# Reordering parts of a hand-scheduled two-layer kernel: gram blocks of the second image, softmax sums, transposes, and identity products at the start

## The chip, the cores and the metric

The kernel runs on one core of one Trainium2 chip. The metric is the device time of one execution in microseconds (us); a figure for a kernel is the median of several runs. TensorE (PE) multiplies, its weight loads (PEld) overlap the products, VectorE (DVE) does elementwise work and statistics, ScalarE (ACT) does exponentials and copies, GpSimd (POOL) does some elementwise work, and SyncE (SP) issues nearly all DMAs in order.

## What is computed

The input x has shape 8 x 768 x 32 x 32, in float32: eight images of 768 channels and 1024 pixels. Two layers follow each other, each with a group norm (`_gn`) ahead of it and a residual sum behind it.

```python
x = x + _L0_conv_ref(_gn(x), W_qkv, W_proj, b_proj)   # layer 0
x = x + _L1_conv_ref(_gn(x), conv_w, conv_b)          # layer 1
...
# layer 0: 12 heads of 64
var_v = jnp.var(v, axis=-1, ddof=1, keepdims=True)
var_k = jnp.var(k, axis=-1, ddof=1, keepdims=True)
attn = softmax(var_v @ swapaxes(var_k) * scale)       # 1024 x 1024 per head
out = (attn @ v) @ W_proj.T + b_proj
...
# layer 1: 28 correlations of the normalised feature with shifts of itself, then a 1x1 convolution
corr = stack([sum(feat_pad[:, :, r:h+r, c:w+c] * feat_n, axis=1) for r, c in offsets])
out = einsum('bchw,oc->bohw', concat([feature, corr]), conv_w) + conv_b
```

The scores are the outer product of two vectors, so the attention matrix of a head is made by exponentials of one row, scaled by one number for each of 128 partitions.

## The kernel before

The program is written out as one static order of instructions for each engine. A planner inside the kernel, `Clock` (L73 to L126), keeps a planned time `now`, planned ends of ACT and DVE work, and a list of jobs with due times. `later.after(us, job)` makes a job due so long after now; `later.after_dve(us, job)` (L89) counts from the planned end of DVE's work. `pass_time` (L110) moves the plan on and emits the jobs that fall due. The plan decides only the order of emission; on the chip each engine runs its own list in that order and waits on semaphores.

**Stages.** For each image b: keys and values (`KeysValues`, 56 units of PE work of 12 matmul records each, L577), attention over six head pairs hp (`Attention`, `Pair`), projection (`project`, L1321), group norm, and layer 1 for the image before (`Corr`, `Conv`), which runs beside the attention of the next image. `work_off` (L1302) takes PE work from three lists: `rest` (key and value units, then convolution units), attention steps in fours, and `beside` (the gram blocks). An entry of `rest` is taken when its keys are in the set `ready`. A step of attention is four blocks t of `products` (L750, matmuls at L756, out tile `av`). Around each such group `next_to(beside)` (L1295) emits one gram block. If both halves of the values are there and the work left in `rest` is at most `TAIL` (L51, 14.0 planned us), that work is held back until attention is over (L1311).

**Softmax sums.** For some pairs (L38, `SUMMED`: pairs 0, 3, 4, 5 for image 0, and 3, 4, 5 for the others) DVE adds the exponentials (`acc`, two buffers of `bkpool`, L174), and PE sums `acc` over the partitions: `sum_up` (L782, tile `den`, L789), and for the last pair `sum_up_last` (L832), which takes reciprocals straight from PSUM in four pieces on DVE (`invert`, L845). For the other pairs ACT sums while it makes a second set of exponentials (`junk`, L741) from a row `bk` that is loaded over 128 partitions; after a summed pair this load is emitted once `bk_free` is set by `sum_up` (L793, L943). The next summed pair may not start before that either (L955).

**Rows for the exponentials.** `spread` (L663) makes the variances on DVE (`vm`, `km`); `values` (L679) then turns them by PE (tile `ptv`, L339), copies them on DVE (`rsv`), and stores them (`vdr`, L551). `rows` (L715) loads each row to 128 partitions (`bc<-vdr`, L720), and the exponentials read it (L731).

**Correlations.** `turn` (L1065) copies one block of the normalised image `f` on POOL (L1078) into the one buffer of `turnpool` (L176); `gram` (L1080) multiplies it with `f` (L1093, 24 records, tile `gr`), copies the result (`win`) and stores it (`windowed`). After blocks 3 and 7 `diagonals` (L1116), `scale` and `columns` take the shifted products from DRAM; `to_dram` (L1147) turns them (tile `ct`) and stores them (`rows<-cr`, L1159); `gather` (L1165) loads them with eleven DMAs into `cs` and `v` (L1170 to L1178). The products and a copy `cs<-cs` (L1187) follow. Some convolution units then get a matmul with `cs` added in the same PSUM bank, two at a time (`join`, L996; L1000). A bank is emptied by DVE (`take`, L1007).

For image 1 (b = 1 in the main loop, whose layer 1 is that of image 0) a fresh `Corr` is made and its first block is turned by the first `gram`. For later images `start_corr` (L1427) turns it ahead, near the end of the first half of keys and values. The gram blocks of b > 1 also get two extra places in `rest`, at indexes 3 and 7 (L1457 to L1458).

Of the kernel before, what the change touches and what calls it, by code (L numbers as in the profile page):

```python
# [6 lines left out]
F32 = mybir.dt.float32  # L7
# [6 lines left out]
P = 128  # L14
# [37 lines left out]
EXP, SUM, STEP_US = 1.07, 1.15, 1.73  # L52
KV_US, T_US, CORR_US = 1.93, 2.58, 1.2
GRAM_US = 1.4

# [100 lines left out]
def two_layers(ctx, tc, x, wkv, wproj, bproj, wconv, wcorr, bconv, out):  # L158
# [225 lines left out]
    sums0 = WeightSums(0, nc.sync, nc.scalar)  # L384
    ident = const.tile([P, P], F32, name="ident")
    make_identity(nc, ident)
    group = const.tile([P, P // 4, 4], F32, name="group")
    nc.gpsimd.memset(group, 0.25)
    for base, sign in ((0, 1), (3, -1)):
# [74 lines left out]
    class Norm:  # L464
# [35 lines left out]
                    nc.scalar.activation(high, high, AF.Identity, bias=shift, scale=self.rstd)  # L500
            ready.add(key)

        def apply(self, to, src, key, apart):


            def chunk(j):
                vector.tensor_scalar(to[:, j, :], src[:, j, :], self.mean, self.rstd, ALU.subtract, ALU.mult)
                if j + 1 < J:
                    later.after(apart, lambda: chunk(j + 1))
                else:  # L510
                    ready.add(key)

            chunk(0)

# [38 lines left out]
    class KeysValues:  # L553
# [109 lines left out]
        def spread(self, half):  # L663
            b = self.b
            name = f"{b}_{half}"
            km2 = st.tile([P, HH, MT], F32, tag="km2", bufs=2, name=f"km2{name}")
            head_m2(self.bn["k", half], km2, f"k{name}")
            top = st.tile([P, HH], F32, tag="top", name=f"top{name}")
            vector.tensor_reduce(top, km2, AX.X, ALU.max)
            most = st.tile([P, HH], F32, tag="most", name=f"most{name}")  # L670
            nc.gpsimd.partition_all_reduce(most, top, P, bass_isa.ReduceOp.max)
            m2 = st.tile([P, HH, MT], F32, tag="vm2", bufs=4, name=f"vm2{name}")
            head_m2(self.bn["v", half], m2, f"v{name}")
            nk = st.tile([P, HH, MT], F32, tag="nk", bufs=4, name=f"nk{name}")
            kdr, vdr = [dpool.tile([HH, N], F32, tag=f"{kind}dr", name=f"{kind}dr{name}") for kind in "kv"]
            for of, new in ((self.m2, m2), (self.nk, nk), (self.kdr, kdr), (self.vdr, vdr)):
                of.append(new)

            def values():  # L679
                to_rows(m2, vdr, f"v{name}")  # L680
                ready.add(("v", b, half))

            def keys():
                for h in range(HH):
                    vector.tensor_scalar(
                        nk[:, h, :], km2[:, h, :], most[:, h : h + 1], HD ** -0.5 / (HD - 1) ** 2,
                        ALU.subtract, ALU.mult,
                    )
                ready.add(("nk", b, half))
                if not set(SUMMED[b > 0]).issuperset(range(3 * half, 3 * half + 3)):  # L690
                    later.after_dve(0.5, rows)

            def rows():
                to_rows(nk, kdr, f"k{name}")
                ready.add(("k", b, half))

            later.after_dve(1.0 if b else 2.5, values)
            later.after_dve(2.2 if b else 3.5, keys)


    class Pair:
# [48 lines left out]
        def products(self, t):  # L750
            if t == 0:
                self.av = avp.tile([P, 2, HF], F32, tag="av", name=f"av{self.b}_{self.hp}")
            exs = self.exs.pop(t)
            for hf in range(2):
                for e in range(2):
                    nc.tensor.matmul(  # L756
                        self.av[e * HD : (e + 1) * HD, hf, :], lhsT=self.vt[:, t, e, :],
                        rhs=exs[e][:, hf * HF : (hf + 1) * HF], start=t == 0, stop=t == MT - 1,
                    )
            if t == MT - 1:  # L760
                later.after(STEP_US + 0.2, self.evacuate)
            if self.summed:
                before = list(self.first)
                if t == 0:
                    self.acc = [bkpool.tile([P, N], F32, tag="bk", name=f"acc{self.b}_{self.hp}_{e}") for e in range(2)]
                for acc, ex in zip(self.acc, exs):
                    if t:
                        vector.tensor_tensor(acc, before.pop(0) if t == 1 else acc, ex, ALU.add)
                self.first = exs
                if t == MT - 1:  # L770
                    later.after_dve(0.5, self.sum_up if self.hp < HP - 1 else self.sum_up_last)
            if t == MT - 1:
                self.over = True
                self.try_finish()
# [57 lines left out]
        def sum_up_last(self):  # L832

            dens = []
            for hf in range(2):
                at = slice(hf * HF, (hf + 1) * HF)
                den = other([P, HF], f"den{self.b}_{self.hp}_{hf}")
                for e in range(2):
                    nc.tensor.matmul(
                        den[e * HD : (e + 1) * HD, :], lhsT=ones, rhs=self.acc[e][:, at], start=True, stop=True  # L840
                    )
                dens.append(den)
            self.rd = self.acc[0]

            def invert(n):  # L845

                q = HF // 2
                vector.reciprocal(self.rd[:, n * q : (n + 1) * q], dens[n // 2][:, n % 2 * q : (n % 2 + 1) * q])
                if n < 3:
                    later.after_dve(1.5 if self.b else 0.0, lambda: invert(n + 1))  # L850
                else:
                    self.rd_at = clock.dve
                    self.try_finish()

            invert(0)

        def invert(self):
            self.inv = invs[self.hp % 2]
# [202 lines left out]
    class Corr:  # L1061
# [70 lines left out]
        def scale(self, hf, dd):  # L1132

            b = self.b
            m = st.tile([P, 4], F32, tag="m", name=f"m{b}_{hf}")
            vector.tensor_scalar(m, dd[:, :, 0], NORM_EPS2, None, ALU.max)
            rn = st.tile([P, 4], F32, tag="rn", name=f"rn{b}_{hf}")
            nc.gpsimd.tensor_tensor(rn, m, neghalf, ALU.pow)

            def columns():  # L1140
                dn = st.tile([P, 4, NROW], F32, tag="dn", name=f"dn{b}_{hf}")
                vector.tensor_copy(dn[:, :, 0], rn)
                for q in range(4):
                    vector.scalar_tensor_tensor(dn[:, q, 1:NROW], dd[:, q, :], rn[:, q : q + 1], mask, ALU.mult, ALU.mult)
                later.after_dve(0.7 if b else 4.0, lambda: to_dram(dn))

            def to_dram(dn):  # L1147
                pt = small(f"ct{b}_{hf}")
                columns, over = dn.rearrange("p q r -> p (q r)"), 4 * NROW - HD
                turned(pt[0:HD, 0:P], columns[:, 0:HD])  # L1150
                turned(pt[HD:P, 0:P], columns[:, over:])
                cr = work([P, P], f"cr{b}_{hf}")
                vector.tensor_copy(
                    cr.rearrange("k (y s x) -> k y s x", y=4, s=2),
                    pt[:, 0:P].rearrange("k (s y x) -> k y s x", s=2, y=4),
                )
                for q in range(4):
                    at, row = PAD + hf * HF + q * P, q * NROW + (HD - over) * (q == 3)
                    nc.sync.dma_start(out=rows[b % 2][:, at : at + P], in_=cr[row : row + NROW, :])  # L1159
                if hf == 1:  # L1160
                    later.after(3.0, self.gather)

            later.after_dve(2.5, columns)
# [138 lines left out]
    def work_off(rest, attention=None, beside=()):  # L1302
        while rest or (attention and not attention.over()):
# [14 lines left out]
            else:  # L1318
                clock.pass_time(0.5)

    def project(b, ots, held=None):  # L1321
        f = first_f[0] if b == 0 else image_tile(fpool, "f", f"f{b}")
        for n, us in ((0, 0.0), (1, 0.5), (3, 1.5), (4, 3.0), (2, 12.0), (5, 14.0)) if b else ():
# [22 lines left out]
        def apply(norm):  # L1346
            to = f if b + 1 < NB else image_tile(xnpool, "xn", "f_last")
            layer1.append((to, f))
            norm.apply(to, f, ("f", b), (2.0 if b else 1.0) if b + 1 < NB else 0.0)

        def spreads_and_apply():
            norms[0].spreads()
# [74 lines left out]
    def start_corr(b):  # L1427
        corrs.append(Corr(b, layer1[b][0]))
        corrs[-1].turn(0)
# [7 lines left out]
    for b in range(NB + 1):  # L1437
# [6 lines left out]
        if b:  # L1444
# [1 line left out]
            if b > 1:  # L1446
                clock.wait(*has_f, ready=ready)
            f, acc = layer1[b - 1] if b > 1 else first_f * 2
            corr = corrs[-1] if 1 < b < NB else Corr(b - 1, f)
            conv = Conv(  # L1450
                b - 1, f, None if b < NB else acc, (lambda b=b: next_image(b + 1)) if b + 1 < NB else lambda: None
            )
            grams = [(GRAM_US if t < MT - 1 else 0.9, has_f, lambda t=t: corr.gram(t)) for t in range(MT)]
            first, start = (0.0, has_f, conv.sums.first), (0.0, (), conv.start)
            if b < NB:
                beside = grams
                for n in (3, 7) if b > 1 else ():  # L1457
                    rest.insert(n, (0.0, has_f, lambda: next_to(beside)))  # L1458
                rest.insert(len(rest) - 4, (0.0, has_f, lambda: remaining(beside)))
                rest.insert(len(rest) - 4, first)  # L1460
# [63 lines left out]
```

## Time and profile before

| | us |
|---|---|
| median of 3 runs (lowest, highest) | 2656.82 (2652.53, 2659.18) |
| the profiled execution: its time | 2655.61 |
| its span, first to last instruction | 2653.9 |
| DVE, ACT, POOL busy | 1605.4, 1368.4, 414.3 |
| exponentials on ACT (L731), x768 | 828.8 |
| attention products on PE (L756), x3072 records | 701.1 |
| chain that ended last: share of PE | 91% |

One float32 matmul call shows as two records in the trace, and two records that fill 64 columns each run side by side. The number in brackets at the end of a row of the timeline is the time for which the engine stood idle ahead of that group, and what ended it; a row merges equal instructions that follow each other, and a row's start is that of its first. `SPq` rows are DMA issues, not transfers. The times of all rows are us from the start of the span.

### The profile page before, as it was taken

The page shows a single profiled execution, that of the slowest core. Times are in us where ns is not written, and L with a number is a line of the kernel's source. Part 1 is how long each engine was busy: PE and PEld are TensorE (multiplying, and loading weights), DVE is VectorE, ACT ScalarE, POOL GpSimd, SP SyncE. Part 2 cuts the span into 40 slices and gives each one's busy share as a digit, 9 for nine tenths or more (in the row PEclk, how much of TensorE's full clock was granted, in tenths as well). Part 3 has the DMA queues.
Part 4 walks back from the last instruction along what each step waited for, and adds up shares of the span by engine and source line. Part 5 has one row for each costly group of instructions (what it writes and reads, how often), then busy time and mean ns, then how long its engine had stood idle before and what let it go on. Part 6 is the DMA issues. An engine that isn't in the chain of part 4 may idle for free.

```text
span 2653.9 us, 40302 instructions
## 1 busy us (share of the span) xinstructions
PE 2602.3 (98%) x14694; PEld 1307.0 (49%) x14694; DVE 1605.4 (60%) x4110; ACT 1368.4 (52%) x1841; POOL 414.3 (16%) x444
## 2 busy tenths in 40 slices
PE   7999999899999999999999999999999999999999
PEld 3554565333674347633466334763347433575333
DVE  6858744676456854478544785348753577535864
ACT  1498069710498215981169801797018960189500
POOL 4320030003210033000430004300123001320000
PEclk9999999999999999999999999999999999999999
DMA  7864455455554555635556364562655526545333
GB/s 287 292 236 147 143 191 144 136 176 168 183 179 135 173 167 180 193 112 195 156 180 196 94 214 154 171 202 80 222 167 165 195 84 230 169 135 167 97 118 101
DMA packets 323391, 446.64 MB, mean 168 GB/s; under 512 B 59458, under 2 KB 245170, under 8 KB 323194
## 3 DMA queue, kind: packets, MB, share of 16 engines
q1 hardware_dynamic: 321962, 441.32, 51.6%
q8 instruction: 117, 1.92, 0.3%
q10 hardware_dynamic: 1232, 2.75, 0.3%
q14 instruction: 80, 0.66, 0.1%
HBM read 377.49 MB, written 64.40 MB: 167 GB/s over the span
## 4 chain that ended last, share of the span: by engine, by line
PE 91%; DMA 4%; DVE 2%; ACT 1%; issue 1%; SPq 1%; POOL 0%; DVEq 0%; POOLq 0%; ACTq 0%
PE x L336 36%; PE av L756 23%; PE y L336 18%; PE z L336 9%; PE gr L1093 3%; DMA x<-x1d 1%; PE den L789 1%; ACT ex L731 1%; PE x L1000 1%; PE y L1000 1%; DMA kv<-kvs 1%; PE z L1000 0%; DMA x1d<-f 0%; DVE x L152 0%; DMA xn<-in_x_dram 0%
## 5 line engine op out<-in xcount | busy, mean ns | idle before, releaser
L731 ACT ACTIVATE ex<-bc,nk 128x1024 f32<-128x1024 f32 x768 | 828.8, 1138 | 422.1 <-DMA bc<-vdr 258.9
L756 PE MATMUL av<-ex,v 128*64 128x512 f32 x3072 | 701.1, 597 | 11.1 <-ACT ex L731 11.1
L756 PEld LDWEIGHTS av<-ex,v 128*64 128x64 f32 x3072 | 322.1, 138 | 345.3 <-issue 206.2
L741 ACT ACTIVATE junk<-bk,vm 128x1024 bf16<-128x1024 f32 x368 | 420.5, 1143 | 31.6 <-DMA bk<-kdr 25.5
L152 DVE TENSOR_TENSOR acc<-acc,ex 128x1024 f32<-128x1024 f32 x300 | 344.6, 1211 | 0.0
L214 ACT COPY kp<-x 128x384 f32<-128x384 f32 x28 | 13.4, 478 | 565.7 <-PE x L336 556.9
L336 PE MATMUL y<-kv,s 128*64 128x384 f32 x1488 | 269.9, 487 | 0.0
L336 PE MATMUL x<-kv,xn 128*64 128x384 f32 x1512 | 265.7, 488 | 1.6 <-DVE xn L152 1.6
L336 PE MATMUL x<-kv,s 128*64 128x384 f32 x1488 | 259.3, 486 | 0.0
L336 PEld LDWEIGHTS x<-kv,xn 128*64 128x64 f32 x1512 | 144.0, 138 | 103.8 <-issue 82.7
L336 PEld LDWEIGHTS x<-kv,s 128*64 128x64 f32 x1488 | 144.2, 137 | 92.1 <-issue 68.8
L336 PEld LDWEIGHTS y<-kv,s 128*64 128x64 f32 x1488 | 140.0, 137 | 87.1 <-issue 68.6
L490 POOL TENSOR_TENSOR rstda<-vea,neghalf 128x1 f32<-128x1 f32 x8 | 4.8, 595 | 978.2 <-DVE vea L152 978.2
L1078 POOL TENSOR_TENSOR turn<-f,ones 128x384 f32<-128x384 f32 x112 | 111.0, 1011 | 257.2 <-PE gr L1093 177.0
L336 PE MATMUL z<-kv,xn 128*64 128x384 f32 x768 | 135.6, 486 | 0.0
L336 PE MATMUL x<-v,wt 128*64 128x512 f32 x576 | 131.1, 594 | 0.0
L336 PE MATMUL x<-f,wt 128*64 128x512 f32 x504 | 119.5, 593 | 0.0
L152 DVE TENSOR_TENSOR v<-y,v 128x128 f32<-128x128 f32 x180 | 41.0, 283 | 127.1 <-PE y L336 127.0
L594 POOL TENSOR_TENSOR s<-xn 128x384 f32<-128x384 f32 x64 | 67.4, 1062 | 285.3 <-PE x L336 192.0
L152 DVE BATCH_NORM_STATS2 vbn<-v 128x6 f32<-128x64 f32 x720 | 101.7, 210 | 0.0
L336 PEld LDWEIGHTS z<-kv,xn 128*64 128x64 f32 x768 | 75.9, 137 | 46.7 <-issue 35.7
L1093 PEld LDWEIGHTS gr<-f,turn 128*64 128x64 f32 x1344 | 90.2, 138 | 16.3 <-POOL turn L1078 5.8
(190 smaller groups left out, 2989.5 us busy)
## 6 DMA issues: line engine op xcount, KB each, us to landing
kv<-kvs SPq DMA_DIRECT2D x124, 576.0 KB
kv<-in_wkv_dram SPq DMA_DIRECT2D x95, 576.0 KB
bc<-vdr SPq DMA_DIRECT2D x96, 512.0 KB
f<-in_x_dram SPq DMA_DIRECT2D x48, 512.0 KB
bk<-kdr SPq DMA_DIRECT2D x46, 512.0 KB
x1d<-f SPq DMA_DIRECT2D x42, 512.0 KB
x<-x1d SPq DMA_DIRECT2D x42, 512.0 KB
out_dram<-x SPq DMA_DIRECT2D x82, 256.0 KB
```

The source lines that it names most:

```text
L152: return getattr(self.engine, name)(*args, **kw)
L214: nc.scalar.copy(to, at)
L336: nc.tensor.matmul(out[at], lhsT=lhsT[:, at], rhs=rhs, start=start, stop=stop, **kw)
L490: nc.gpsimd.tensor_tensor(self.rstd, ve, neghalf[:, 0:1], ALU.pow)
L594: nc.gpsimd.tensor_tensor(self.sums[g][:, 0], a[g][2], a[g][3], ALU.add)
L731: nc.scalar.activation(ex, self.bc[e], AF.Exp, scale=self.kv.nk[self.half][:, h, t : t + 1])
L741: nc.scalar.activation(junk, self.bk[e], AF.Exp, scale=self.kv.m2[self.half][:, h, t : t + 1], accum_out=self.sums[:, e, t : t + 1],)
L756: nc.tensor.matmul(self.av[e * HD : (e + 1) * HD, hf, :], lhsT=self.vt[:, t, e, :], rhs=exs[e][:, hf * HF : (hf + 1) * HF], start=t == 0, ...
L789: nc.tensor.matmul(den[at * 32 : (at + 1) * 32, :], lhsT=ones[:, 0:32], rhs=self.acc[e][:, hf * HF : (hf + 1) * HF], start=True, stop=True,)
L1000: nc.tensor.matmul(t, lhsT=wcorr_sb[at, i, :], rhs=cs[at, tokens, :], start=False, stop=True, skip_group_check=True)
L1078: nc.gpsimd.tensor_tensor(to[:, :, side], half, windows(ones, ones.ap[0], (0, J), (HW, 4), (1, HW)), ALU.mult)
L1093: nc.tensor.matmul(ps[side * HD : (side + 1) * HD, :n].rearrange("p (y x) -> p y x", x=WIDE), lhsT=block[:, j, side, :], rhs=image[:, 4 * ...
```

## The change

Eight edits, none of which adds or removes arithmetic of the result.

1. 36 matmuls of the identity with itself (128 x 128) into a scratch bank, right after the identity is made.
2. For image 0, the end of the normalisation of `f` (`Norm.apply`) calls `turn_first`: `start_corr(0)` turns gram block 0 on POOL, and six planned us later the key "turned" becomes ready. The gram blocks of b = 1 need that key besides `("f", 0)`.
3. The gram blocks of b = 1 get extra places in `rest`, at indexes 7, 11 and 15.
4. For image 0, `to_dram` is due 0.7 us behind DVE's work rather than 4.0.
5. For image 0 and pairs other than the last, `sum_up` is due 3.0 us behind DVE's work rather than 0.5.
6. For images after 0, the first reciprocal of the last pair is due 1.2 us after `sum_up_last` rather than at once.
7. For b > 1 and the second half of keys and values, `values` and `keys` are due 1.0 us later.
8. `corrs[-1]` becomes `corrs.pop()`, since the list is now also filled for image 0.

```diff
+WARM = 36
...
     make_identity(nc, ident)
+    warm = smp.tile([P, 512], F32, tag="sm", name="warm")
+    for n in range(WARM):
+        nc.tensor.matmul(warm[:, 0:P], lhsT=ident, rhs=ident, start=True, stop=True)
...
-        def apply(self, to, src, key, apart):
+        def apply(self, to, src, key, apart, then=None):
...
                     ready.add(key)
+                    if then:
+                        then()
...
-            later.after_dve(1.0 if b else 2.5, values)
-            later.after_dve(2.2 if b else 3.5, keys)
+            more = 1.0 if b > 1 and half else 0.0
+            later.after_dve((1.0 if b else 2.5) + more, values)
+            later.after_dve((2.2 if b else 3.5) + more, keys)
...
-                    later.after_dve(0.5, self.sum_up if self.hp < HP - 1 else self.sum_up_last)
+                    last = self.hp == HP - 1
+                    later.after_dve(0.5 if self.b or last else 3.0, self.sum_up_last if last else self.sum_up)
...
-            invert(0)
+            later.after(1.2 if self.b else 0.0, lambda: invert(0))
...
-                later.after_dve(0.7 if b else 4.0, lambda: to_dram(dn))
+                later.after_dve(0.7, lambda: to_dram(dn))
...
+    def turn_first():
+        start_corr(0)
+        later.after(6.0, lambda: ready.add("turned"))
...
-            norm.apply(to, f, ("f", b), (2.0 if b else 1.0) if b + 1 < NB else 0.0)
+            norm.apply(to, f, ("f", b), (2.0 if b else 1.0) if b + 1 < NB else 0.0, None if b else turn_first)
...
-            corr = corrs[-1] if 1 < b < NB else Corr(b - 1, f)
+            corr = corrs.pop() if 1 < b < NB else Corr(b - 1, f) if b == NB else None
...
-            grams = [(GRAM_US if t < MT - 1 else 0.9, has_f, lambda t=t: corr.gram(t)) for t in range(MT)]
+            grams = [(GRAM_US if t < MT - 1 else 0.9, has_f if b > 1 else has_f + ("turned",), lambda t=t: (corr or corrs[0]).gram(t)) for t in range(MT)]
...
-                for n in (3, 7) if b > 1 else ():
+                for n in (3, 7) if b > 1 else (7, 11, 15):
                     rest.insert(n, (0.0, has_f, lambda: next_to(beside)))
```

## The prediction, made before the changed kernel was run

> **What bounds the kernel now.** I read the page's busy shares first, then the list of who waited for whom on PE, then the timeline around each wait.
>
> ```profile
> PE 2602.3 (98%) x14694; PEld 1307.0 (49%) x14694; DVE 1605.4 (60%) x4110; ACT 1368.4 (52%) x1841; POOL 414.3 (16%) x444
> ```
>
> PE is the bound almost everywhere: only 2653.9 − 2602.3 = 51.6 us of the span are not PE's, 13.9 of them ahead of its first instruction. No edit removes PE work, so a gain can only come from those gaps and from slow PE work after them. The waits:
>
> ```profile
> PE pma L336 <- DVE mva L152: 13.9, 1, 13.9
> PE av L756 <- ACT ex L731: 11.1, 4, 4.5
> PE x L336 <- DVE x L152: 4.8, 6, 1.1
> PE gr L1093 <- POOL turn L1078: 4.7, 2, 4.4
> PE ptv L339 <- DVE vm L152: 3.4, 4, 1.9
> PE den L789 <- DVE acc L152: 2.6, 1, 2.6
> ```
>
> Columns: total, times, longest. Each edit has its line here, 40.5 us in all, of which the first 13.9 end with the statistics of the first image and no edit moves those. The rest is 26.6 us. On top comes the granted clock, by stretches of the profile:
>
> ```profile
> 245.00:248.50 3.50, 1.05 (x4) 0.14 (x4) 3.50 (x4) 3.50 (x6) 0.00 (x0) 1.00 0.44 123
> 248.50:252.00 3.50, 3.42 (x9) 0.72 (x10) 2.65 (x4) 2.05 (x2) 0.00 (x0) 0.51 0.00 0
> 357.80:364.50 6.70, 4.45 (x28) 3.65 (x30) 5.17 (x29) 3.35 (x6) 2.65 (x3) 0.50 0.34 127
> 470.40:477.20 6.80, 5.31 (x12) 2.55 (x14) 1.31 (x2) 6.42 (x7) 0.00 (x0) 0.50 1.01 382
> 484.10:487.40 3.30, 2.99 (x7) 1.36 (x9) 3.30 (x5) 3.30 (x5) 0.00 (x0) 0.50 0.00 0
> ```
>
> The second number is PE's busy time, the third from the end the clock. After each wait of 2.6 us or more PE runs at half clock, so half of its busy time there is lost as well.
>
> **The gram copy (edits 2, 3).** Around 355 us:
>
> ```profile
> 357.84 0.81 DVE L152 TENSOR_SCALAR f<-f,meanb,rstdb 128x1024 f32<-128x1024 f32 x1 [7.34 <-DMA x1d<-f]
> 358.73 1.97 POOL L1078 TENSOR_TENSOR turn<-f,ones 128x384 f32<-128x384 f32 x2 [14.15 <-DVE f L152]
> 359.79 0.71 PE L1093 MATMUL gr<-f,turn 128*64 128x133 f32 x2 [4.43 <-POOL turn L1078]
> ```
>
> POOL had been idle for 14.15 us, so emitting its copy sooner starts nothing sooner: `f` itself is late, behind the store `x1d<-f`. What helps is "turned". The planner's arithmetic decides the order of emission (never the time); followed through for before, it says: `("f", 0)` is ready at 344.9 planned us, the first attention group is taken at 350.4 with gram 0 ahead of it. "Turned" comes at 350.9, just too late, so attention goes first and gram 0 behind it. Worth: 4.43 + 0.26 idle and 4.45 / 2 = 2.2 of half clock, 6.9. What is late next: attention now starts at 355.1 and reaches block t = 3 at 360.3 (1.73 a step). ACT has six exponentials done at 357.5, then two `junk` of 1.27 ahead of the next pair, which ends at 357.5 + 2.5 + 2.1 = 362.1: a wait of some 1.4. Net −5.5. Bounds: −6.9, and 0 if "turned" is ready in time and nothing swaps. The three places put grams one key unit (1.93) apart, and the single turn buffer needs 0.1 + 1.97 after each gram: about 0.2 us each for three, +0.5.
>
> **The gather (3, 4).** Around 450 us:
>
> ```profile
> 450.50 0.92 SPq L1170 DMA_DIRECT2D cs<-rows  x1
> ...
> 462.26 0.36 SPq L551 DMA_DIRECT2D vdr<-rsv  x1
> ```
>
> ```profile
> 470.69 4.47 ACT L731 ACTIVATE ex<-bc,nk 128x1024 f32<-128x1024 f32 x4 [9.44 <-DMA bc<-vdr]
> ```
>
> `rsv` was copied at 452.9, but SP sat in the eleven issues of the gather from 450.5 to 460.4, several of them waiting, and issued the store at 462.3; the rows (`bc`) wait for it and are issued at 466.7. ACT then waits 9.44 us for the rows, and PE twice for ACT: 4.47 and 3.90 us, with half of 5.31 and 2.99 lost to the clock: 8.4 + 4.1 = 12.5. In the planned order of before, `gather` stands 2.8 us ahead of `values`. With the extra places gram 7 goes from 409.1 to about 402.2 planned, and edit 4 takes 3.3 off, so `gather` stands some 13 us ahead. That is the distance of the later images (12.9), and there the same steps read: last gather issue 775.3, `vdr` 785.5, `bc` 787.1, with no PE wait on ACT at all. So most of it goes. Left over: ACT has four `junk` between the third and fourth exponential pair of that head pair, for which I leave 1.5, and the wait of `ptv` for `vm` that the later images have and this one hardly has, 0.7. Net −10.3; bounds −12.5 and 0. What SP does sooner: the eleven gather DMAs and the four stores of edit 4 now pass key and value loads. Five weight blocks are buffered, of two units each, some 15 us of cover against 10 us of issues; without it PE would wait the difference.
>
> **The sums of image 0 (5).**
>
> ```profile
> 128.72 1.15 ACT L741 ACTIVATE junk<-bk,vm 128x1024 bf16<-128x1024 f32 x1 [7.38 <-DMA bk<-kdr]
> 131.68 0.64 PE L756 MATMUL av<-ex,v 128*64 128x512 f32 x1 [1.57 <-ACT ex L731]
> ```
>
> Here one `junk` was put ahead of the exponentials of t = 3; it waits on ACT for `bk`, and PE waits behind it. With `sum_up` 2.5 later, the load of `bk` and the `junk` come after the exponentials of t = 3 and 4: −1.6 idle and some 0.4 at its edges, −2.0. Pair 4's `den` (2.60 idle, clock 0.51 over 3.42) stays: the seven units left are 13.5 us, under the 14.0 of `TAIL`, so nothing is emitted between, and PE waits for DVE's sums, which the edit doesn't shorten. Pair 3's `den` comes a unit later, which holds the two `acc` buffers 1.9 longer but moves that unit's DVE work out of a later 2.0 us gap: 0 net, bounds −3 and +3.
>
> **The reciprocals (6).**
>
> ```profile
> 889.68 1.76 DVE L152 RECIPROCAL acc<-den 128x256 f32<-128x256 f32 x1 [4.18 <-PE den L839]
> 893.76 2.79 PE L336 MATMUL x<-t4f,wt 128*64 128x512 f32 x12 [0.73 <-DVE x L152]
> ```
>
> DVE waits for `den`, does a reciprocal, then the update of `v`, then empties the joined banks, and PE waits for one of them: six images, 4.8 us. But the planner of before has `join` at 855.9, `sum_up_last` at 857.1 and the banks' emptying 3.9 after the join, at 859.8. The reciprocal moves to 858.3, still ahead. The order on DVE stays, so 0; bounds −4.8 and +1.
>
> **The transposes (7).** In before, `values` is due 0.17 planned us after attention block t = 2 of pair 2, and block 3 follows at 1.73. At 1.17 it still stands between the same two blocks, for every b > 1. PE's order doesn't change; only DVE's copy `rsv` moves behind three sums (1.88). 0; bounds −3.4 and +1.
>
> **The identity products (1).** The nearest row is `ct`, four records of 128 columns:
>
> ```profile
> 404.75 0.49 PE L339 MATMUL ct<-ident,dn 128*64 128x128 f32 x3
> ```
>
> With the fourth at 405.08 that is 0.11 a record, 0.22 a product, 0.43 at half clock. The identity is made at 1.6; with half clock at first the 36 end at about 11 to 13, ahead of PE's first real instruction at 13.86. The first products (16.97) now run at 0.64 a pair against 0.32, until about 20: 1.5 us to win. [...] the row at 245 to 248.5 is sharper: 2.45 us idle in a stretch of 3.5, and half clock followed. From 11 to 13 until 16.97 PE has only eight one-column records, a gap of 4 to 6 us, so by the row the clock is gone again: 0. I take the row. Bounds −1.5, and +3.2 if all run at half clock (36 x 0.43 = 15.4, ending at 17.0).
>
> **Sum.** −5.5 + 0.5 − 10.3 − 2.0 = −17.3. Against the profiled execution's 2655.6 that is 2638.3; the median of the runs shown is 1.2 higher. I say 2638.
>
> **The rivals.**
> - All edits do what they are named for: 4.8 of the reciprocals and 3.4 of the transposes come off too, and 1.5 at the start: 2628. For it: each has its wait in the list. Against it: the orders above. 0.15.
> - The rows for the exponentials stay late for another reason (the four `x<-x1d` loads of 512 KB, 4.47 us of DVE wait in a later image): half of the 12.5 stays and the wait on `ptv` grows: 2647. 0.15.
> - Waits are only exchanged: attention starts sooner and waits for ACT, pair 4 for DVE: 2654. 0.06.
> - Slower, by the identity products alone: their weights fill 128 columns, twice any load in this trace. If a load (0.137 for 64 columns, 0.232 at half clock in the first products) isn't hidden behind a product, a record costs up to 0.21 + 0.46 = 0.67, and 72 end at 50, 36 us late: 2674. It decides from 0.8 us a product: (12.3 + 17.3) / 36. Against it: loads of 64 columns are wholly hidden in `ct`. 0.04.
> - The forecast, 2631 to 2645: 0.60.
>
> A measurement tells 0.3% (8 us) from no change. Faster than 2648.8: 0.60 + 0.15 + half of the second rival's 0.15 = 0.82; within: 0.14; slower: 0.04. The range, 2626 to 2650, takes in the second case whole and most of the third.
>
> **What would show it.** The wait of `gr` on `turn` gone, with `av` ahead of the first gram; gather issues ended 10 us before `vdr<-rsv`, and no clock of 0.50 near 470 and 484; the wait of `av` at 131.7 gone, that of `den` at 247 still there; `x` on DVE and `ptv` on `vm` as before in the later images; the first `x` records still 0.64 apart. I'd be wrong if `ptv` or `x<-t4f` waits vanish, if `pma` starts after 14, or if key units wait for `kv` loads near 430.

## The result, and the profile after

The changed kernel takes 2642.39 us (median of 6 runs, 2639.91 to 2645.02); the kernel before, on the same chip, 2655.34 (2652.53 to 2659.18). The ratio is 0.9951, with a 95% interval of 0.9939 to 0.9964: about 13 us faster, where 17 to 19 were forecast (2638). The profiled execution's span is 2638.7 us against 2653.9, so 15.2 less; its time, 2640.4, lies 2 us under the median, which is why the two differences differ.

First the busy shares of the page, then the list of who waited for whom on PE (total, times, longest), both of the changed kernel. Lines have moved by 1 to 8: L337 was L336, L763 was L756.

```profile
PE 2610.0 (99%) x14766; PEld 1318.2 (50%) x14766; DVE 1604.3 (61%) x4110; ACT 1367.3 (52%) x1841; POOL 413.6 (16%) x444
```

PE has 72 records more than before (14694), two for each of the 36 identity products. Records of 64 columns can begin two at a time: in before two at 30.35 us, the next two 0.32 us later.

```profile
PE x L337 <- DVE x L153: 4.6, 6, 0.9
PE ct L340 <- DVE dn L153: 3.3, 1, 3.3
PE av L763 <- ACT ex L738: 3.2, 2, 2.4
PE ptv L340 <- DVE vm L153: 2.3, 3, 1.2
...
PE den L797 <- DVE acc L153: 1.0, 1, 1.0
...
PE gr L1101 <- POOL turn L1086: 0.5, 2, 0.2
```

The wait of `gr` for `turn` is gone (4.7 to 0.5), that of `av` for `ex` is cut from 11.1 to 3.2, that of `den` from 2.6 to 1.0. `x` and `ptv` still wait in the later images. `pma` waits 1.3 instead of 13.9, only because the identity products fill the time ahead of it; it starts at 13.88, as before. New is a wait of `ct` for `dn` of 3.33 us.

The stretches around it, from the changed kernel's table by window (PE busy is the second number, the granted clock the third from the end):

```profile
392.90:396.30 3.40, 0.60 (x6) 0.45 (x8) 1.08 (x7) 3.37 (x5) 1.83 (x2) 1.00 0.07 27
396.30:399.70 3.40, 3.40 (x15) 1.58 (x13) 0.17 (x1) 3.40 (x5) 0.00 (x0) 0.50 0.07 17
```

After the start, two waits are still followed by half clock: this new one, and what is left of the wait for the exponentials (2.45 us of idle time, half clock from 478.2 to 481.6). The stretches at 248, 358 and 484 of before have no half clock any more (1.00 there).

How PE stands against before, at the start of the same instruction: at image 0's second group norm (`pmb`) 336.71 against 341.25, 4.5 ahead; at the first attention product of image 2, 691.89 against 705.63, 13.7 ahead; at the end 15.2. So image 0 gave 4.5, the stage with the second image's grams and gather 9.2, and the six later images 1.5.

### The profile page after: what moved, and what is told of

Read it like the earlier page. It is cut to its first block, busy times and chain, and to the rows that moved or that the text cites. A ratio compares the mean times of both kernels' runs of the same rounds, so it can differ in the third digit from the quotient of the medians.

```text
span 2638.7 us, 40466 instructions
## 1 busy us (share of the span) xinstructions
PE 2610.0 (99%) x14766; PEld 1318.2 (50%) x14766; DVE 1604.3 (61%) x4110; ACT 1367.3 (52%) x1841; POOL 413.6 (16%) x444
## 4 chain that ended last, share of the span: by engine, by line
PE 89%; DMA 3%; ACT 3%; DVE 2%; issue 1%; SPq 1%; POOL 1%; DVEq 0%; ACTq 0%; POOLq 0%
PE x L337 35%; PE av L763 22%; PE y L337 17%; PE z L337 9%; PE gr L1101 3%; ACT ex L738 1%; ACT junk L748 1%; DMA x<-x1d 1%; DMA v<-rows 1%; DMA bc<-vdr 1%; PE x L1008 1%; PE den L797 1%; PE y L1008 1%; PE z L1008 1%; DVE acc L153 1%
## 5 line engine op out<-in xcount | busy, mean ns | idle before, releaser
L763 PE MATMUL av<-ex,v 128*64 128x512 f32 x3072 | 700.2, 596 | 3.4 <-ACT ex L738 3.2
L763 PEld LDWEIGHTS av<-ex,v 128*64 128x64 f32 x3072 | 316.6, 137 | 339.0 <-issue 210.5
L337 PE MATMUL y<-kv,s 128*64 128x384 f32 x1488 | 269.4, 487 | 0.0
L337 PE MATMUL x<-kv,xn 128*64 128x384 f32 x1512 | 264.3, 489 | 1.6 <-DVE xn L153 1.6
L337 PE MATMUL x<-kv,s 128*64 128x384 f32 x1488 | 258.2, 486 | 0.0
L337 PEld LDWEIGHTS x<-kv,xn 128*64 128x64 f32 x1512 | 145.3, 138 | 101.1 <-issue 80.5
L337 PEld LDWEIGHTS x<-kv,s 128*64 128x64 f32 x1488 | 145.2, 137 | 91.2 <-issue 67.6
L337 PEld LDWEIGHTS y<-kv,s 128*64 128x64 f32 x1488 | 140.7, 137 | 87.1 <-issue 69.2
L337 PE MATMUL z<-kv,xn 128*64 128x384 f32 x768 | 135.1, 486 | 0.0
L337 PE MATMUL x<-v,wt 128*64 128x512 f32 x576 | 131.1, 594 | 0.0
L337 PE MATMUL x<-f,wt 128*64 128x512 f32 x504 | 120.1, 594 | 0.0
L337 PEld LDWEIGHTS z<-kv,xn 128*64 128x64 f32 x768 | 76.4, 137 | 45.9 <-issue 34.3
```

Source lines behind the costliest of these rows:

```text
L337: nc.tensor.matmul(out[at], lhsT=lhsT[:, at], rhs=rhs, start=start, stop=stop, **kw)
L763: nc.tensor.matmul(self.av[e * HD : (e + 1) * HD, hf, :], lhsT=self.vt[:, t, e, :], rhs=exs[e][:, hf * HF : (hf + 1) * HF], start=t == 0, ...
```

## The experiments

All start from the changed kernel, but for the last. The theory after the result: the missing 4 us are the new wait of `ct`, made by edit 4 behind POOL's queue. The rival: the extra gram places make it.

| kernel | median us | ratio to before (95%) | profiled span |
|---|---|---|---|
| changed kernel | 2642.39 | 0.9951 (0.9939 to 0.9964) | 2638.7 |
| ct of first half at 4.0 again | 2635.78 | 0.9936 (0.9924 to 0.9948) | 2633.6 |
| ct of both halves at 4.0 | 2634.34 | 0.9930 (0.9914 to 0.9945) | 2634.5 |
| no extra gram places | 2644.19 | 0.9960 (0.9948 to 0.9972) | 2642.5 |
| sums of image 0 at 0.5 | 2644.94 | 0.9966 (0.9954 to 0.9978) | 2643.2 |
| no identity products | 2639.67 | 0.9938 (0.9925 to 0.9950) | 2637.7 |
| identities up to first product | 2644.12 | 0.9951 (0.9938 to 0.9963) | 2639.2 |
| reciprocals at 3.2 | 2679.13 | 1.0087 (1.0073 to 1.0101) | 2677.4 |
| transposes 2.0 later | 2637.41 | 0.9927 (0.9914 to 0.9941) | 2635.7 |
| "turned" at once | 2645.18 | 0.9962 (0.9948 to 0.9976) | 2643.7 |
| both ct at 4.0, transposes 2.0 | 2630.44 | 0.9909 (0.9896 to 0.9923) | 2628.4 |
| the same, identities in an own bank | 2629.64 | 0.9907 (0.9893 to 0.9920) | 2626.9 |
| before with "turned" alone | 2647.20 | 0.9970 (0.9959 to 0.9980) | 2646.9 |

Intervals of kernels that lie less than some 0.0025 apart overlap, so a small difference can't be told from these ratios alone. What decides there is the trace: which wait is there or gone, and how far PE is at the start of the same instruction.

### Edit 4 undone, in part and whole

```diff
-                later.after_dve(0.7, lambda: to_dram(dn))
+                later.after_dve(0.7 if b or hf else 4.0, lambda: to_dram(dn))
```

> The changed kernel with edit 4 undone for the first half of the correlations alone (due 4.0 us behind DVE's work again; the second half keeps 0.7). Theory: the changed kernel misses the forecast because PE waits 3.33 us for dn (DVE's copy waits for rn, which POOL has queued behind the shifted sums s and a turn), and runs some 3.4 us at half clock after it; with ct back behind a block of attention products and gram 6 that wait is hidden: 5.0 us faster than the changed kernel, about 2637, ratio to before 0.993, no wait of ct over 0.5 us, no half clock near 396, and the issues of the gather where the changed kernel has them (431 to 437), less the 5 us. Rival: the wait comes from the extra places of the grams (edit 3), which put the sums and turns on POOL ahead of rn; then PE waits somewhere else and the time stays within 1.5 us of 2642.

```diff
-                later.after_dve(0.7, lambda: to_dram(dn))
+                later.after_dve(0.7 if b else 4.0, lambda: to_dram(dn))
```

> The changed kernel with edit 4 undone for both halves. Theory: as with the first half alone, the wait of ct on dn goes (5.0 us), and the second half's four stores and so the eleven issues of the gather come some 3 us later, still ahead of the store of the value rows; at most 1 us of PE's waits for exponentials comes back: 2637 to 2639. Rival (the prediction's step for the gather, which counted edit 4's 3.3 us as part of what brings the gather ahead): the rows are late again by 3 us and the waits for exponentials grow by 3 to 4: 2640 to 2642, nothing gained against the changed kernel.

Measured: spans 5.1 and 4.2 us shorter than the changed kernel's, ratios 0.9936 and 0.9930 against 0.9951, with intervals that overlap. In the stage from 337 to 692 us both win 15.3 us on before, the changed kernel 9.2. The timeline of the changed kernel shows what PE waited for:

```profile
384.09 1.96 POOL L600 TENSOR_TENSOR s<-xn 128x384 f32<-128x384 f32 x2
...
391.77 1.96 POOL L1086 TENSOR_TENSOR turn<-f,ones 128x384 f32<-128x384 f32 x2
393.71 1.02 POOL L1146 TENSOR_TENSOR rn<-m,neghalf 128x4 f32<-128x4 f32 x1
394.76 0.17 DVE L153 COPY dn<-rn 128x4 f32<-128x4 f32 x1 [7.20 <-POOL rn L1146]
...
395.70 0.44 PE L340 MATMUL ct<-ident,dn 128*64 128x128 f32 x4 [3.33 <-DVE dn L153]
```

`rn` is an instruction of 1 us, but it stands on POOL behind 9.6 us of other work, four rows of shifted sums and a turn, without a gap from 384.09 on. Its own input `m` is written on DVE by 387.03, so 6.7 us of that queue are pure delay. DVE stands 7.20 us in front of it and PE 3.33. With both halves late:

```profile
395.45 1.94 PE L1101 MATMUL gr<-f,turn 128*64 128x133 f32 x23
396.40 0.17 DVE L153 COPY dn<-rn 128x4 f32<-128x4 f32 x1 [7.21 <-POOL rn L1146]
...
398.27 0.44 PE L340 MATMUL ct<-ident,dn 128*64 128x128 f32 x4 [0.37 <-DVE ir L153]
```

DVE waits as long as before, 7.21, but PE does an attention block and gram 6 meanwhile. The theory holds. The second kernel also fells the rival expectation, that the gather needs edit 4: its issues begin at 432.05 instead of 431.01, `vdr<-rsv` at 447.0 instead of 449.3, and the wait of `av` near 473 is 0.89 instead of 2.45 us. Nothing is lost by undoing edit 4 altogether.

### The extra places of the grams

```diff
-                for n in (3, 7) if b > 1 else (7, 11, 15):
+                for n in (3, 7) if b > 1 else ():
```

> The changed kernel with edit 3 undone (no extra places for the gram blocks of the second image). Theory: the extra places are what brings the gather ahead of the store of the value rows, so without them the gather's issues end near or behind the time at which that store is wanted (some 7 us later than the changed kernel's 437), and most of PE's wait for exponentials and of the half clock near 470 and 484 comes back: 6 to 10 us slower than the changed kernel, 2648 to 2652. Rival: edit 2 with edit 4 is enough for it, since attention is 5 us sooner: within 2 us of 2642; and if the extra places also make the new wait of ct on dn, it is gone here and the time is 2637.

Measured: span 3.8 us longer, medians 1.8 apart (the intervals overlap), less than the 6 to 10 expected. Both sides of it were right in part. The gather comes late again; SP's issues in this kernel, and who waits:

```profile
456.51 0.47 SPq L557 DMA_DIRECT2D vdr<-rsv  x1
...
465.27 8.48 PE L763 MATMUL av<-ex,v 128*64 128x512 f32 x24 [4.30 <-ACT ex L738]
```

The store of the value rows leaves SP right behind the last of the eleven issues (456.12), and half clock from 463.4 to 470.2 (0.51 and 0.50 by window) goes with PE's 4.30. But `ct` no longer waits for `dn`. So the wait of `ct` takes edits 3 and 4 together, and undoing 4 alone keeps the gain: from 337 to 692 us the changed kernel wins 9.2 us on before, this one 7.3, and the kernels with edit 4 alone undone 15.3.

### The gram copy by itself

```diff
-        later.after(6.0, lambda: ready.add("turned"))
+        later.after(0.0, lambda: ready.add("turned"))
```

> The changed kernel with the key "turned" set at once instead of 6.0 planned us later; the turn on POOL is emitted as early as in the changed kernel, but grams 0 and 1 now stand ahead of the first attention products on PE. Theory: the gain at the gram copy comes from the order on PE alone, since f, not POOL, is what is late; with the gram ahead PE waits for the turn again, and longer than before's 4.43 us because gram 0 now stands a key unit earlier: 7 to 12 us slower than the changed kernel, 2650 to 2654, and a wait of gr for turn over 4 us in all. Rival: the earlier turn on POOL is what helped; no such wait, within 1 us of 2642.

Span 5.0 us longer, medians 2.8 apart. The wait is there, and longer than in before: `gr` waits for `turn` 11.7 us in all and 7.8 at a time. The longest one, with half clock from 349.0 to 359.3 (21 records of `gr` take 2.70 us from 355.62, and 23 take 1.66 from 360.51), makes PE 7.2 us later than the changed kernel at attention record 425 (377.08 against 369.87), as expected. At the first attention product of image 2 it is 6.3 us later, and 5.1 at the end; it regains the 1.3 us between in later images, in which the two kernels have the same order of instructions. The copy on POOL starts at 353.6 here and 353.8 in the changed kernel: it is the order on PE that gained. The expected total of 7 to 12 was too large.

> The kernel of before with edits 2 and 8 alone: the turn emitted at the end of the normalisation of f and the key "turned" 6.0 planned us later. Theory (the prediction's step): this swaps gram 0 behind the first attention block and is worth 5.5 us at that place (waits of 4.43 and some half clock gone, a small wait of av for ex instead), and since the gather stands no sooner than in before, the waits of av for ex near 460 to 485 stay: 2650, ratio 0.998. Rival: with attention 5 us sooner and the gather where it was, the waits there grow by as much and nothing is left: 2655.

(The kernel of before with edits 2 and 8.) Measured 2647.2, the span 7.0 under before's: faster than the theory's 2650, and the rival, that waits are only exchanged, falls. Attention first, the gram behind it, and a wait of 0.77 for ACT where 1.4 was forecast (its timeline):

```profile
361.43 2.54 PE L760 MATMUL av<-ex,v 128*64 128x512 f32 x7 [0.77 <-ACT ex L735]
363.38 0.62 PE L1098 MATMUL gr<-f,turn 128*64 128x133 f32 x4
```

By attention record 425 this kernel is 7.0 us ahead of before, counted from the second group norm (372.14 − 341.40 against 378.98 − 341.25). Near 460 to 480 its waits for exponentials remain (3.64 and 2.49).

### The sums of image 0

```diff
-                    later.after_dve(0.5 if self.b or last else 3.0, self.sum_up_last if last else self.sum_up)
+                    later.after_dve(0.5, self.sum_up_last if last else self.sum_up)
```

> The changed kernel with edit 5 undone (sums of image 0 due 0.5 us behind DVE's work again). Theory from the two traces: the whole gain of 4.5 us that PE has by 337 us is of this edit (the wait of av at 131.7 with 2.0, and some 2.5 of the wait of den near 245 with the half clock behind it): 4.5 us slower, 2647, with both waits back. Rival (the prediction's step): only 2.0 of it is, the rest is of another edit (the pop or the turn), so 2644.4 and the wait of den stays at 1.0.

Span 4.5 us longer, medians 2.6. Both waits are back, as this kernel's timeline shows; the first wait of PE stands behind a `junk` that waited for `bk`, as in before:

```profile
133.49 3.01 PE L763 MATMUL av<-ex,v 128*64 128x512 f32 x6 [2.43 <-ACT ex L738]
...
241.27 0.69 DVE L153 TENSOR_TENSOR vs<-y,vs 128x128 f32<-128x128 f32 x3 [2.01 <-PE y L337]
...
250.81 2.20 PE L797 MATMUL den<-acc,ones 128*32 128x512 f32 x6 [2.60 <-DVE acc L153]
```

The same place in the changed kernel:

```profile
244.43 2.19 PE L797 MATMUL den<-acc,ones 128*32 128x512 f32 x8 [0.98 <-DVE acc L153]
```

So the second wait belongs to this edit too, and the traces show what moved. With the sums early, a key and value unit stands on PE between the two halves of pair 4 (239.12 to 241.05 here, 235.76 to 237.69 in before). DVE waits 2.01 us for its product `y` in the middle of pair 4's sums and then does that unit's work, to 242.64. In the changed kernel the unit comes ahead of pair 4 (its `vs` at 227.83), PE runs all 64 records of pair 4 in a row from 228.51, and DVE adds without that stop. PE keeps full clock behind `den` (1.00 from 245.0 to 252.0).

At 337 us this kernel is 7.2 us behind the changed one. Of this 0.7 are from the clock at the very start, and some 1.7 from half clock behind the first wait (2.43 us; half clock from 134.2 to 137.7), which before, where PE waits 1.57 us, does not have (1.00 from 19.8 to 248.5). It gains some back later, where its wait for exponentials is 1.78 and not 2.45.

### The identity products

```diff
-    for n in range(WARM):
-        nc.tensor.matmul(warm[:, 0:P], lhsT=ident, rhs=ident, start=True, stop=True)
```

> The changed kernel without the identity products at the start (edit 1 undone). Theory (the prediction's): PE stands idle for over 4 us between the last of them and the first long product, so the clock is gone again by then and they are worth nothing: within 0.5 us of the changed kernel (2642), and the first key products 0.64 us a pair of records in both until the clock rises some 3.4 us after they begin. Rival[...]: 1.5 us slower without them, 2644.

Measured 2639.67, not slower. The start of the first attention product shows that the 36 products gain nothing that can be told from the clock's own scatter: it comes at 95.9 to 97.8 us in the nine kernels that have just these 36 products (96.29 in the changed one), and at 96.1, 96.1 and 97.5 in the three without (before, before with "turned" alone, and this one). What differs from one to the next, with or without them, is when the half clock at the start ends: between 19.6 and 23.1 us.

So this kernel is 1.2 us behind the changed one there, and yet 1.0 us ahead at the end. The reason lies later. Its `ct` waits the same 3.33 us, up to 396.68, but the clock stays at 1.00:

```profile
391.30:394.70 3.40, 2.04 (x10) 0.77 (x6) 0.00 (x0) 3.40 (x4) 3.40 (x5) 1.00 0.49 154
394.70:398.10 3.40, 1.42 (x10) 0.79 (x12) 1.25 (x7) 3.37 (x6) 1.01 (x2) 1.00 0.00 0
398.10:401.50 3.40, 3.40 (x39) 2.85 (x37) 0.48 (x2) 3.37 (x5) 1.16 (x2) 1.00 0.05 12
```

In the changed kernel half clock from 396.27 to 399.68 followed the same idle time and cost some 1.7 us more (half of 3.41). Why it came in one kernel and not in the other is not shown.

> The changed kernel with 42 identity products at the start instead of 36, three more behind the first group product (pma) and seven behind the second (pva), into unused columns of the same banks, so that PE has no gap of over some 1 us before the first key product. Theory: the clock is kept by products that reach to the first real one, so it stays full there and the first key products run at 0.32 a pair from 17.0 on instead of from 20: 1.5 us faster than the changed kernel, 2641 (profile: no half clock from 17 to 21). Rival: [...]half clock from 17 to 21 as before, 2642 to 2643.

(Its edit, for the first group norm only: `if name == "a0":` and three, then seven products `pm[:, P : 2 * P]`, `pv[:, P : 2 * P]` of `ident` with `ident` behind `pma` and `pva`.) No gain in total, ratio 0.9951; but the clock was kept. PE's rows:

```profile
14.15 0.94 PE L482 MATMUL pma<-ident 128*128 128x128 f32 x6
...
19.56 4.09 PE L337 MATMUL x<-kv,xn 128*64 128x384 f32 x24 [1.64 <-DVE xn L153]
```

24 records take 3.9 us to the next row (23.48), at full clock; in the changed kernel 5.6 (16.87 to 22.49). What was won was lost again, since DVE's reads of `pma` and `pva` waited for the products in the same tiles: `pva` starts 1.94 us behind `pma` and the first key product 3.68 behind `pva`, where the changed kernel has 1.08 and 1.91. So that product came at 19.56, 2.7 us late. A version with a bank of its own stands below.

### The reciprocals and the transposes at delays that move them

```diff
-            later.after(1.2 if self.b else 0.0, lambda: invert(0))
+            later.after(3.2 if self.b else 0.0, lambda: invert(0))
```

> The changed kernel with the first reciprocal of the last pair due 3.2 us after the sums instead of 1.2, so that in the order of DVE the reciprocals do stand behind the emptying of the joined banks. Theory: edit 6 does nothing because 1.2 us leaves the reciprocals ahead of the banks; with 3.2 the wait of x<-t4f for DVE (0.72 to 0.9 us, six images) goes: 4.3 us faster than the changed kernel, 2638. Rival: the later reciprocals make the last pair's values late, and the projection waits for them; PE's waits only change their name, and the time stays within 1 us of 2642 or is above it.

37 us slower. The theory was wrong; the rival ("or is above it") had the direction, but nothing near the size. The wait of `x` for DVE's `x` fell from 4.6 to 0.8 us as hoped; in its place PE waits for `t2o` 29.4 us in all, and half clock follows in each of the six images (mean clock 0.991 in this profile, 0.998 in the changed kernel's). The first of these images in this kernel's timeline, where six records of `x<-t2o` take 2.83 us (eight take 1.89 in the changed kernel):

```profile
893.73 0.75 DVE L153 SCALAR_TENSOR_TENSOR f<-x,bproj_sb,f 128x512 f32<-128x512 f32 x1 [6.25 <-DMA f<-in_x_dram]
894.39 1.75 DVE L153 RECIPROCAL acc<-den 128x256 f32<-128x256 f32 x1
...
897.76 1.89 DVE L153 TENSOR_TENSOR t2o<-v,t1o 128x512 f32<-128x512 f32 x3
...
898.50 2.83 PE L337 MATMUL x<-t2o,wt 128*64 128x512 f32 x6 [5.72 <-DVE t2o L153]
```

The last reciprocal now stands behind a second `f`, which waits 6.25 us for the load of `f`. In the changed kernel it starts at 888.63, ahead of that `f`, and PE's products with `t2o` at 893.65. Edit 6 at its 1.2 leaves PE's order of instructions exactly as it is without the edit; in these six images it moves on DVE only the last reciprocal past one `f`.

```diff
-            more = 1.0 if b > 1 and half else 0.0
+            more = 2.0 if b > 1 and half else 0.0
```

> The changed kernel with the transposes of the value and key rows delayed by 2.0 us instead of 1.0 for the later images, so that ptv stands behind one more block of attention products on PE. Theory: edit 7 does nothing because 1.0 leaves ptv between the same two blocks; with 2.0 the wait of ptv for vm (2.3 to 3.6 us in all over the later images) goes: 2 to 3 us faster, about 2640. Rival: the value rows are stored 2 us later, and the exponentials of the next pair 0 wait for them; 2642 or slower, with new waits of av for ex in the later images.

Faster: span 3.0 less, ratio 0.9927 (its interval still touches that of the changed kernel, 0.9951). The wait of `ptv` for `vm` fell from 2.3 us in three places to 1.2 in one, and no wait of `av` for `ex` of over 0.2 us came in its place. Edit 7 at 1.0 leaves PE's order unchanged; at 2.0 `ptv` goes behind one more block.

### The best of it together

> The changed kernel with edit 4 undone for both halves and the transposes 2.0 us later: the two changes that gained by themselves. Theory: they act at different places, so the gains add: the wait of ct for dn gone (4 to 5 us) and the waits of ptv for vm in the later images too (2 to 3): 2633 to 2636, ratio to before about 0.992, better than either alone. Rival: they overlap (the gain of the second was a difference from run to run), so it is no better than ct alone: 2635 to 2637.

2630.44 us (2629.87 to 2631.35): the gains add. Against the changed kernel it is 0.42% less, with intervals that don't meet. Its list of waits has neither `ct` for `dn` nor `ptv` for `vm`; that of `x` for DVE is still there (4.3 us, six times), and that of `av` for `ex` is 1.5.

```diff
-WARM = 36
+WARM = 44
...
-    warm = smp.tile([P, 512], F32, tag="sm", name="warm")
-    for n in range(WARM):
-        nc.tensor.matmul(warm[:, 0:P], lhsT=ident, rhs=ident, start=True, stop=True)
+    warm = avp.tile([P, 2, HF], F32, tag="av", name="warm")
+    def identities(count):
+        for n in range(count):
+            nc.tensor.matmul(warm[:, 0, 0:P], lhsT=ident, rhs=ident, start=True, stop=True)
+    identities(WARM)
...
+            if name == "a0":
+                identities(2)
...
+            if name == "a0":
+                identities(5)
```

> The kernel of e10 with 44 identity products at the start, two behind pma and five behind pva, all into a PSUM bank that nothing else uses at that time, so that DVE's reads of pma and pva don't wait for them as they did in e8. Theory: PE has no long gap from 1.6 to 17, the clock stays full, the first key product starts at 17.0 as in the changed kernel (not at 19.6 as in e8), and the first 24 records take 4.1 us instead of 5.5 to 6.9: 1.4 to 2 us less than e10 by PE's 25th record of the attention of image 0. Rival: the clock falls all the same (half clock from 17 to 21), nothing gained.

PE's rows at the start:

```profile
15.67 1.38 PE L392 MATMUL warm<-ident 128*128 128x128 f32 x10
17.38 4.09 PE L337 MATMUL x<-kv,xn 128*64 128x384 f32 x24 [0.33 <-DVE xn L153]
```

The first key product comes 0.4 us later than in the kernel that this one starts from (the 44 ran until 14.5 and held `pma` up; from `pma` to `pva` it is 0.99 us, from there to this product 1.93), its 24 records take 3.9 us, and from then on PE is 1.25 us ahead (first attention product 95.11 against 96.36, and earlier than in any of the twelve kernels counted above). The span is 1.5 less; the medians, 2629.64 and 2630.44, can't tell that apart. It is the fastest version seen here by its profile.

## Why the prediction was right in direction and 4 us short

Faster was right, and the mechanisms mostly were. The sum of −17.3 became −15.2 in the profile: 6.1 us were lost by a wait that the prediction did not have, and 2.5 (sums of image 0) and 1.5 (later images) gained more than forecast. That the total lies so near is in part luck.

- **Gram copy.** Right in mechanism (order on PE, not POOL's start). Size −5.5; alone it gave 7.0. One term that was too large is the 1.4 us left for ACT (its own times, 362.1 and 360.3, would even make 1.8); 0.77 was measured. The other 0.9 us of the difference I can't place.
- **Edit 4's wait: the step that failed.** The prediction counted the stores of edit 4 on SP, but costed its earlier `ct` at nothing and never asked when `dn` is ready. It asked what is late next at the gram copy, not here. In before `ct` stood so late (404.75) that POOL's queue ahead of `rn` was hidden; taking 3.3 planned us and several gram units away uncovered 3.33 us idle and some 1.7 of half clock. Undoing edit 4 showed the price: in the stage from 337 to 692 us, 15.3 instead of 9.2 us, so 6.1 with what follows from it.
- **Gather.** Right that the issues end well ahead of the store of `vdr` (437 against 449). That the 15.3 us with `ct` late are just what the prediction's terms for this stage give (−5.5 + 0.5 − 10.3) is luck, since the copy gave more and the gather less, some 8: as the changed kernel stands, PE still waits 2.45 us for the exponentials, and half clock follows, 4.1 us against the 1.5 left for it. That edit 4's 3.3 us are part of what brings the gather ahead was wrong: without them it is as good.
- **Sums of image 0.** −2.0 forecast, −4.5 measured. The step that failed here: pair 4's `den` was said to stay, because the edit doesn't shorten DVE's sums. Its wait fell from 2.60 to 0.98, and no half clock follows. The prediction had seen that a unit's DVE work leaves a 2.0 us gap, but set this at 0 (bounds 3 either way).
- **Reciprocals and transposes.** 0 each. PE's order is unchanged by both, as forecast, but no run undoes either by itself, so 0 is not shown. That the rival counted their waits as gains (4.8 and 3.4) is half true: the transposes' can be had with another delay; the one other delay tried for the reciprocals took their wait away and cost 37 us.
- **Identity products.** 0, right: half clock from 17.39 to 20.80, just as the first key products run. That a gap of 4 to 6 us loses the clock was an estimate from one row of before; the two kernels with products up to the first key product have its 24 records in 3.9 us rather than 5.6. Their own 36 ran from 1.6 to 12.6, so the slower rival, from 0.8 us a product, was far off at 0.3. It said that no load in the trace of before is as wide; the convolution's `cs` products do load 128 columns there, in 0.18 us each.
- **Later images.** 0 forecast, 1.5 measured. Eight kernels that have the same order of instructions in this part, the changed one among them, gain 0.3 to 2.7 there on before; the one without edits 6 and 7 (before with "turned" alone) gains 0.1. So the gain may belong to these two edits, through DVE and the DMA issues, whose order they do change; which of them, and by what wait, stays open.

## What to carry to other kernels

When an instruction is moved ahead on the busiest engine, follow its inputs through every queue they pass: here a small one in the middle (a power of 1 us on GpSimd) started 6.7 us after its input was ready, behind other work of that engine, which is busy for 16% of the span. A delay in a plan does something on an engine only where it moves an instruction of that engine past another; whether it does can be seen by comparing the two orders before any run. And the identity products gained here only where they reached to the first key product in a tile of their own, 1.25 us at the start; those that ended at 12.6 gained nothing that shows, and those in the tiles of `pma` and `pva` brought that product 2.7 us late.

## What the runs showed of the hardware

Half clock stands in the trace of before at 248.53 to 251.94, 357.75 to 364.58, 470.39 to 477.22 and 484.05 to 487.46 us, at waits of PE of 2.60, 4.43, 4.47 and 3.90 us. In the changed kernel it stands at 17.39 to 20.80, at 396.27 to 399.68 (a wait of 3.33) and at 478.19 to 481.60 (2.45). Waits of 1.57 us (before, at 131.68) and of 0.74 and 0.98 (changed kernel, at 356.71 and 244.43) had none. The length of a wait does not tell it alone: one of 3.33 us had half clock behind it in the changed kernel and none in the one without identity products. What else decides is not shown.

Runs of one kernel show the clock and the span together: the changed kernel's six go from 2638.2 us at a mean clock of 0.999 to 2643.3 at 0.997. That the clock alone makes this difference is not shown.

The clock column reads 1.00 as long as a trace has no record of the clock yet. In before the first is at 19.83, and the column reads 1.00 from 16.9 to 20.0, where PE's 10 records take as long as 22 in the next 3 us; there the length of the products tells.
